# Two attention layers on one core: sums of a chunk held for a later stage, halves added by products with ones, TensorE kept busy during the first loads, and four units in the first group of scores

## The chip, the cores and the metric

The kernel runs on one core of one Trainium2 chip. The metric is the device time of one execution in microseconds (us). Several executions of each kernel were timed; "median" is over those. The span that the profile gives is about 2 us shorter than the time, because it runs from the first to the last instruction of the core. The granted clock is the share of full speed that the profile shows for TensorE's clock, 1.00 or less. PE is TensorE, PEld its weight loads, DVE is VectorE, ACT is ScalarE, POOL is GpSimd.

## The reference, cut to what matters

The input has 8 images of 64 channels and 64 x 64 = 4096 positions. Each passes through two attention layers, and all of it is in fp32.

```python
# layer 0 of one image, n = 4096 positions
f = einsum('oc,bcn->bon', Wf, xf) + bf          # 8 channels
g = einsum('oc,bcn->bon', Wg, xf) + bg          # 8 channels
hh = einsum('oc,bcn->bon', Wh, xf) + bh         # 64 channels
beta = softmax(einsum('bci,bcj->bij', f, g), axis=2)
x = x + einsum('bcj,bij->bci', hh, beta)
# layer 1
xn = group_norm(x)                              # 8 groups
q, k, v = split(w_qkv @ xn + b_qkv)             # 64 channels each
out = softmax(q k^T * c**-0.5) v
x = w_proj @ out + b_proj + x
```

So there are 16 attentions of 4096 x 4096. The division by the sum of the exponentials is done at the end, once for each chunk of queries.

## The kernel before: the parts that matter

A layer of an image is four chunks of 2 x 512 queries; a chunk is 16 key tiles; a key tile is four units, each a score product of 128 keys with 512 queries in one PSUM bank. TensorE makes the scores, ScalarE exponentiates them into one of six buffers, TensorE weighs the values with the exponentials, and VectorE adds the exponentials of each tile into a running sum. Layers are run in the order layer 0 of image 0, layer 0 of image 1, layer 1 of image 0, layer 0 of image 2, layer 1 of image 1 and so on, so only at the beginning do two layers 0 follow each other.

```python
def weigh(i, j, e, cols, now):
    ...
    at.weigh(acc, e[:, p], t, p, j == 0, j == 2 * NT - 1, cols)
    ...
    if t == 0:
        first = e
    else:
        added = vector.tensor_add(esum, first if t == 1 else esum, e).ins   # 128x2048
    if t == NT - 1:
        finished(i, now)
```

At the end of a chunk the running sum, which still has two halves p = 0 and 1, becomes one sum for each query. There are two ways. One adds the halves on VectorE and sums over the partitions by a product with ones on TensorE. The other, for chunks that are "held", is done later, on VectorE, in the next layer-1 stage; a held sum needs a buffer of its own until then.

```python
def holds(self, c):
    return self.kind == 0 and self.b > 0 and c < (1 if self.b == 1 else NC - 1)

def halves():
    ...
    vector.tensor_add(esum[:, 0], esum[:, 0], esum[:, 1])

def sums(spare):
    for h in range(2):
        for i in range(2):
            matmul(z[row : row + 32, 0:width], ones[:, 0:32],
                   esum[:, 0, h, ts(i, width)], start=True, stop=True, ...)
    nc.scalar.copy(zs, z[:, 0:width])
    ...   # four small DMAs bring the sums to 128 partitions

def finished(i, now):
    ...
    if at.kind == 1 or next_kind == 1 or held:
        ...   # halves, transposed, reciprocals, result: in the next stage
        return
    behind(halves)()
    ...       # sums, reciprocals, result: 7, 11 and 15 tiles later
```

At the start, the first 512 columns of image 0 are projected directly (`project_direct`), the other columns of the first pair of chunks by `project(0, (1,))`, and the second pair by `rest` at step 0. The first copy of values is on VectorE, all others are on ScalarE. Layer 1 needs the group norm's reciprocal root of a variance, which VectorE finds by four steps of Newton's iteration (`deviations`).

Of the kernel before, what the change touches and what calls it, by code (L numbers as in the profile page):

```python
# [9 lines left out]
F32 = mybir.dt.float32  # L10
# [58 lines left out]
def fast_path(  # L69
# [51 lines left out]

    made_last = {}
    added = None
    tight = False

    def in_order(made, engine="tensor"):

# [22 lines left out]
    def matmul(*args, **kwargs):  # L150
        in_order(nc.tensor.matmul(*args, **kwargs))  # L151

    def behind(work_):


        def made():
            with tc.issue_after(added):
                work_()

        return made  # L160
# [22 lines left out]
        return t  # L183


    w1 = const.tile([P, 2, C8], F32, name="w1")
    for i, (w, queue) in enumerate(((WfT, nc.scalar), (WgT, nc.sync))):
        for h in range(2):
# [24 lines left out]
    with tc.issue_after(masked):  # L213
# [10 lines left out]
        wfg = const.tile([P, 2, 4, C8], F32, name="wfg")  # L224
        nc.vector.tensor_copy(wfg, w1.unsqueeze(2).broadcast_to([P, 2, 4, C8]))
    wfg = wfg.rearrange("p i s c -> p (i s c)")
    fgb_low = const.tile([P, 2], F32, name="fgb_low")
    fgb, lowmask = fgb_low[:, 0:1], fgb_low[:, 1:2]
    for j in range(2):
# [20 lines left out]
    nc.vector.tensor_single_scalar(odd, lane, 1, op=ALU.bitwise_and)  # L250
    lowmask32 = const.tile([P, 1], F32, name="lowmask32")
    nc.vector.tensor_scalar(lowmask32, odd, -1.0, None, op0=ALU.mult)
    ones = const.tile([P, C], F32, name="ones")
    nc.vector.memset(ones, 1.0)


    QP = 2 * CW // P
# [67 lines left out]
    class Attention:  # L325
# [7 lines left out]

        def holds(self, c):

            return self.kind == 0 and self.b > 0 and c < (1 if self.b == 1 else NC - 1)

        def values(self, src, w, c):

            ps = pair()  # L340
            for t in range(TPC):
                for m in range(2):
                    for h in range(2):
                        matmul(
                            ps[ts(m, C), h, ts(t, C)], src[ts(h, C), ds(t * P + m * C, C)],
                            w[ts(h, C), :], start=True, stop=True,
                        )

            copy = vector.tensor_copy if self.kind == self.b == c == 0 else nc.scalar.copy
            copy(  # L350
                self.vt[:, :, ts(c, TPC), :],
                ps[:, :, 0 : TPC * C].rearrange("k p (t c) -> k p t c", c=C),
            )

        def finish(self, acc, esum, c, index):

            n = f"{self.name}_{c}"
            raw = work.tile([P, CW], F32, tag="raw", bufs=4, name=f"raw_{n}")
            other = self.total(raw, acc, index)
            zt = small.tile([P, QP], F32, tag="zt", bufs=4, name=f"zt_{n}")  # L360
            width = CW // 2
            r = four = None

            def halves():
                if other is not None:
                    vector.tensor_add(raw, raw, other)
                vector.tensor_add(esum[:, 0], esum[:, 0], esum[:, 1])

            def transposed():


                nonlocal four
                both_ = work.tile([P, 8 * QP], F32, tag="zs", name=f"part_{n}")
                part = both_[:, 0:32]
                four = both_[:, 32:].rearrange("p (a k) -> p a k", k=QP)
                vector.tensor_reduce(
                    part, esum[:, 0].rearrange("p h (i b) -> p b (h i)", b=32),
                    axis=AX.X, op=ALU.add, apply_transpose=True,
                )
                for a in range(4):  # L380
                    nc.sync.dma_start(four[:, a, :], part[ts(a, 32), :])

            def sums(spare):

                z = banks[:, spare, :]

                zs = work.tile([P, width], F32, tag="zs", name=f"zs_{n}")
                for h in range(2):
                    for i in range(2):
                        row = 32 * (2 * h + i)  # L390
                        matmul(
                            z[row : row + 32, 0:width], ones[:, 0:32], esum[:, 0, h, ts(i, width)],
                            start=True, stop=True, tile_position=(0, row),
                        )
                nc.scalar.copy(zs, z[:, 0:width])
                for h in range(2):
                    for i in range(2):
                        row = 32 * (2 * h + i)
                        nc.sync.dma_start(zt[row : row + 32, :], zs[row : row + 1, :])  # L399

            def broadcast():
                nonlocal r
                r = work.tile([P, CW], F32, tag="r", name=f"r_{n}")

            def reciprocals():
                rt = stash[:, ts(index, QP)]
                if four is not None:
                    vector.tensor_reduce(
                        zt, four.rearrange("p a k -> p k a"), axis=AX.X, op=ALU.add
                    )  # L410
                vector.reciprocal(rt, zt)
                broadcast()
                dealt = recips[index]
                nc.sync.dma_start(dealt, rt)
                for h in range(2):
                    row = dealt[ts(h, C), :].rearrange("p e -> (p e)")
                    nc.sync.dma_start(r[ts(h, C), :], row.partition_broadcast(C))

            def result():
                vector.tensor_mul(raw, raw, r)  # L420
                self.residual(raw, c)

            return halves, transposed, sums, reciprocals, result
# [52 lines left out]
    class Layer0(Attention):  # L476
# [4 lines left out]
        def before(self):  # L481



            def begin():
                if self.b == 1:
                    self.own(F32R)
                else:
                    self.parts = proj.tile([P, 2, NH], F32R, tag="fg", name=f"fg_{self.name}")
                    if self.b != 2:  # L490
                        self.own_vt()
                self.f, self.g = self.parts[:, 0, :], self.parts[:, 1, :]
                self.st = small.tile(
                    [P, NC, nc.vector.BN_STATS_DIM], F32, tag="st", name=f"st_{self.name}"
                )
                if self.b > 0:
                    self.project_all()
                else:
                    self.project_direct()
                    self.project(0, (1,))  # L500

            def rest():
                self.project(1)
                with tc.issue_after(self.sent.ins):
                    for b in (1, 2):
                        load_x(b)

            if self.b == 0:
                return [(-1, begin, True), (0, rest, True)] + [
                    (  # L510
                        (-1, 1, 5, 8)[c],
                        lambda c=c: self.values(x_tiles[0][:, ts(c, CW)], wh, c),
                        True,
                    )
                    for c in range(NC)
                ]



            s, spread = (28, 32) if self.b == 1 else (0, 28)  # L520
            return [(s, begin, True), (spread, self.spread, False)] + [
                (
                    (36, 38, 43, 45)[c],
                    lambda c=c: self.values(x_tiles[self.b][:, ts(c, CW)], wh, c),
                    True,
                )
                for c in range(NC)
            ]
# [4 lines left out]
        def home(self, c):  # L533

            if self.b > 1:
                if c == 0:
                    layers1[self.b].own(F32)
                return layers1[self.b].parts[:, c, :]
            layers0[2].own_vt()
            return layers0[2].vt.rearrange("q p t c -> q (p t c)")  # L540

        def project_direct(self):

            ps = pair()
            full = work.tile([P, 2, CW], F32, tag="full", bufs=1, name="full_direct")
            high = work.tile([P, 2, CW], F32R, tag="high", bufs=1, name="high_direct")
            for i, dst in enumerate((self.f, self.g)):
                matmul(
# [110 lines left out]
    class Layer1(Attention):  # L659
# [8 lines left out]
        def before(self):  # L668
# [32 lines left out]
            def deviations():  # L701
# [8 lines left out]
                )  # L710
                y = guess.bitcast(F32)
                w = small.tile([P, 1], F32, tag="w", name=f"w_{n}")
                for i in range(4):
                    vector.scalar_tensor_tensor(w, y, y, ve, op0=ALU.mult, op1=ALU.mult)
                    vector.tensor_scalar(w, w, -0.5, 1.5, op0=ALU.mult, op1=ALU.add)
                    vector.tensor_mul(y, y, w)
# [179 lines left out]
    def finished(i, now):  # L896
# [7 lines left out]
        if at.kind == 1 or next_kind == 1 or held:  # L904
# [4 lines left out]
            for s, u in ((0, halves), (1, transposed), (5, reciprocals), (8, result)):  # L909
                at_step(when + s, behind(u), 0)  # L910
            return
        behind(halves)()

        spare = outer[c % 2 if at.kind == 0 else 1]
        delay = 7 if at.kind == 0 else 5
# [35 lines left out]
    while i < len(seq):  # L951
# [32 lines left out]
        while u < len(units):  # L984
# [13 lines left out]
            if taken == PAIR:  # L998
                lent = 0 if room[-1] == 7 else 2
                room = [r for r in room if r not in (2 * lent + 1, 2 * lent + 2)]  # L1000
            group = list(zip(units[u : u + len(room)], room))
            u += len(group)
            for (k, t, p, h), bank in group:
# [411 lines left out]
```

## Time and profile before

| before | |
|---|---|
| median time | 3005.99 us (3005.14 to 3006.30, 4 runs) |
| span of the profile | 3004.0 us |
| first scores | 14.40 us |
| fourth group of scores | 27.20 us |
| first scores of layer 1 of image 0 | 338.95 us |
| first layer 0 after a layer 1 | 562.59 us |

Layer 1 of image 0, where the timeline has its first scores (`banks<-kq_l` of 64 x 64):

```profile
338.95 3.66 PE L151 MATMUL banks<-kq_l 64*64 64x512 f32 x32
```

The stretch between the fourth group and that mark, as one window (length, then busy us of PE, PEld, DVE, ACT, POOL, then granted clock, DMA share, GB/s):

```profile
27.20:338.95 311.75, 302.27 (x2099) 110.11 (x2097) 294.41 (x175) 251.79 (x227) 0.00 (x0) 1.00 0.11 28
```

TensorE has 9.48 us without work in it (311.75 less 302.27).

### The profile page before, as it was taken

The page shows a single profiled execution, that of the slowest core. Times are in us where ns is not written, and L with a number is a line of the kernel's source. Part 1 is how long each engine was busy: PE and PEld are TensorE (multiplying, and loading weights), DVE is VectorE, ACT ScalarE, POOL GpSimd, SP SyncE. Part 2 cuts the span into 40 slices and gives each one's busy share as a digit, 9 for nine tenths or more (in the row PEclk, how much of TensorE's full clock was granted, in tenths as well). Part 3 has the DMA queues.
Part 4 walks back from the last instruction along what each step waited for, and adds up shares of the span by engine and source line. Part 5 has one row for each costly group of instructions (what it writes and reads, how often), then busy time and mean ns, then how long its engine had stood idle before and what let it go on. Part 6 is the DMA issues. An engine that isn't in the chain of part 4 may idle for free.

```text
span 3004.0 us, 58286 instructions
## 1 busy us (share of the span) xinstructions
PE 2973.7 (99%) x25629; PEld 1078.7 (36%) x25629; DVE 2574.0 (86%) x1659; ACT 2073.0 (69%) x2019; POOL 16.1 (1%) x40
## 2 busy tenths in 40 slices
PE   8999999999999999999999999999999999999998
PEld 3333333333333333333333333333333333333333
DVE  7999986899878998789986999879997799976776
ACT  6888656786567866678666785668856688566554
POOL 2000000000000000000000000000000000000000
PEclk9999999999999999999999999999999999999999
DMA  2100100101001010010100102000020000000000
GB/s 65 43 8 15 47 16 19 30 1 44 20 20 29 1 45 19 21 28 1 49 19 20 26 1 51 16 23 22 1 52 20 19 8 1 17 24 15 9 16 13
DMA packets 77141, 66.93 MB, mean 22 GB/s; under 512 B 54048, under 2 KB 54080, under 8 KB 75088
## 3 DMA queue, kind: packets, MB, share of 16 engines
q1 hardware_dynamic: 75792, 63.01, 8.7%
q8 instruction: 202, 3.31, 0.5%
q14 instruction: 59, 0.48, 0.1%
q0 software_dynamic: 768, 0.09, 0.0%
q10 hardware_dynamic: 320, 0.04, 0.0%
HBM read 39.84 MB, written 12.32 MB: 17 GB/s over the span
## 4 chain that ended last, share of the span: by engine, by line
PE 93%; DVE 4%; issue 1%; ACT 1%; DMA 0%; SPq 0%; DVEq 0%; ACTq 0%
PE banks L151 93%; DVE esum_l L141 3%; DVE vt_l L141 1%; ACT e_l L1013 1%; DMA x<-in_x_dram 0%; DVE x L141 0%; DVE raw_l L141 0%; DVE st_l L141 0%; ACT full_l L573 0%; DVE high_l L141 0%; DVE kq_l L141 0%; DVE rt L141 0%; SPq L399 0%; DMA zt_l<-zs_l 0%; DVE w_l L141 0%
## 5 line engine op out<-in xcount | busy, mean ns | idle before, releaser
L141 DVE TENSOR_TENSOR esum_l<-esum_l,e_l 128x2048 f32<-128x2048 f32 x629 | 1438.9, 2288 | 272.0 <-ACT e_l L972 246.3
L972 ACT ACTIVATE e_l<-banks 128x1024 f32<-128x1024 f32 x1024 | 992.2, 1022 | 680.6 <-PE banks L151 680.6
L151 PE MATMUL banks<-e_l,v_l 64*64 64x512 f32 (+1 forms) x8780 | 1090.2, 586 | 0.0
L1013 ACT ACTIVATE e_l<-banks 128x2048 f32<-128x2048 f32 (+3 forms) x727 | 953.8, 1373 | 183.5 <-PE banks L151 165.9
L151 PE MATMUL banks<-kq_l 64*64 64x512 f32 (+1 forms) x8448 | 1004.4, 585 | 6.5 <-ACT e_l L1013 5.7
L151 PE MATMUL banks<-e_l,vt_l 128*64 128x512 f32 (+1 forms) x4056 | 829.8, 550 | 0.0
L141 DVE TENSOR_TENSOR kq_l<-kq_l,e_l 128x2048 f32<-128x2048 f32 x252 | 577.5, 2292 | 24.4 <-ACT e_l L1013 0.5
L151 PEld LDWEIGHTS banks<-e_l,v_l 64*64 64x64 f32 (+1 forms) x8780 | 346.9, 133 | 589.3 <-issue 490.0
L151 PEld LDWEIGHTS banks<-kq_l 64*64 64x64 f32 (+1 forms) x8448 | 326.2, 134 | 602.9 <-issue 561.8
L151 PEld LDWEIGHTS banks<-e_l,vt_l 128*64 128x64 f32 x4056 | 267.8, 136 | 467.7 <-issue 447.6
L151 PE MATMUL banks<-fg_l 32*128 32x512 f32 x1792 | 204.7, 459 | 6.2 <-ACT e_l L1013 3.1
L141 DVE TENSOR_TENSOR esum_l<-e_l,e_l 128x2048 f32<-128x2048 f32 x45 | 102.3, 2274 | 86.2 <-ACT e_l L972 86.2
L151 PEld LDWEIGHTS banks<-fg_l 32*128 32x128 f32 x1792 | 84.8, 183 | 186.8 <-ACT e_l L1013 139.8
L141 DVE TRANSPOSE_TENSOR_REDUCE part_l<-esum_l 128x32 f32<-128x1024 f32 x38 | 74.7, 1967 | 0.0
L141 DVE TENSOR_TENSOR esum_l<-esum_l 128x1024 f32<-128x1024 f32 x44 | 53.7, 1220 | 0.4
L141 DVE TENSOR_TENSOR raw_l<-raw_l,r_l 128x512 f32<-128x512 f32 x63 | 43.2, 685 | 2.1 <-DMA r_l<-recips 2.1
L141 DVE TENSOR_TENSOR kq_l<-e_l,e_l 128x2048 f32<-128x2048 f32 x18 | 41.1, 2283 | 0.0
L651 ACT COPY raw_l<-banks 128x512 f32<-128x512 f32 x32 | 18.9, 590 | 25.2 <-PE banks L151 24.3
L141 DVE TRANSPOSE_TENSOR_REDUCE part_l<-kq_l 128x32 f32<-128x1024 f32 x18 | 35.2, 1955 | 0.0
L141 DVE TENSOR_TENSOR vt_l<-vt_l,e_l 128x2048 f32<-128x2048 f32 x14 | 32.1, 2291 | 1.2
L764 ACT ACTIVATE kq_l<-banks,kqb 64x256 f32<-64x256 f32 x64 | 30.1, 470 | 1.2
L151 PEld LDWEIGHTS banks<-wh,x 64*64 64x64 f32 x1024 | 21.2, 138 | 16.7 <-issue 15.8
(127 smaller groups left out, 467.9 us busy)
## 6 DMA issues: line engine op xcount, KB each, us to landing
r_l<-recips SPq DMA_DIRECT2D x126, 128.0 KB
kq_l<-kq_l SPq DMA_DIRECT2D x64, 128.0 KB
out_dram<-raw_l SPq DMA_DIRECT2D x62, 128.0 KB
x<-in_x_dram SPq DMA_DIRECT2D x30, 256.0 KB
fg_l<-fg_sent_l SPq DMA_DIRECT2D x24, 256.0 KB
fg_l<-fg_sent_l SPq DMA_DIRECT2D x48, 128.0 KB
part_l<-part_l SPq DMA_DIRECT2D x228, 4.0 KB
fg_sent_l<-high_l SPq DMA_DIRECT2D x28, 128.0 KB
```

Source lines behind the costliest of these rows:

```text
L141: it = getattr(nc.vector, name)(*args, **kwargs)
L151: in_order(nc.tensor.matmul(*args, **kwargs))
L651: nc.scalar.copy(raw, acc[0])
L764: nc.scalar.activation(self.q[ts(h, C), cols[1]], ps[other, 1, 0:width], AF.Identity, bias=k1["kqb"][other, :],)
L972: nc.scalar.activation(e[:, p], both_ps[p], AF.Exp, scale=at.scale)
L1013: nc.scalar.activation(e.rearrange("k p h n -> k (p h) n")[:, first_ : first_ + n_, :], banks[:, bank : bank + n_, :], AF.Exp, scale=at.scale,
```

## The change

Five things are changed. (1) The two halves of a sum are no longer added on VectorE ahead of the product with ones; the product accumulates over both. (2) The first three chunks of image 1 are held in place of the first alone, two of them in a buffer that belongs to a projection later. (3) Newton's iteration takes three steps. (4) At the start, TensorE multiplies ones and weights into a bank that nobody reads until x has come; the copy of the first values goes to ScalarE; the tile of the direct projection gets another buffer; the second projection is asked for at step 2; and VectorE's instructions are held in program order (`tight`) ahead of the first chunk too (both kernels hold them so in the first eight chunks). (5) The first group of scores of a layer 0 that follows a layer 1 has four units in place of six.

```diff
-    tight = False
+    tight = True
...
+    def warm(rows, n):
+        for i in range(n):
+            matmul(banks[0:C, 7, 0:C], rows, rows, start=True, stop=True)
+    warm(ones, 18)
...
+    warm(wfg, 10)
...
-            return self.kind == 0 and self.b > 0 and c < (1 if self.b == 1 else NC - 1)
+            return self.kind == 0 and self.b > 0 and c < NC - 1
...
-            copy = vector.tensor_copy if self.kind == self.b == c == 0 else nc.scalar.copy
-            copy(
+            nc.scalar.copy(
...
-                        matmul(z[row : row + 32, 0:width], ones[:, 0:32],
-                               esum[:, 0, h, ts(i, width)], start=True, stop=True, ...)
+                for p in range(2):
+                            matmul(z[row : row + 32, 0:width], ones[:, 0:32],
+                                   esum[:, p, h, ts(i, width)],
+                                   start=p == 0, stop=p == 1, ...)
...
-                return [(-1, begin, True), (0, rest, True)] + [
+                return [(-1, begin, True), (2, rest, True)] + [
...
+            if c == 1:
+                self.free = proj.tile([P, 2, NH], F32, tag="fg", name="free")
+            return self.free[:, c - 1, :]
...
-            full = work.tile([P, 2, CW], F32, tag="full", bufs=1, name="full_direct")
+            full = ppool.tile([P, 2, 2, CW], F32, tag="e", name="full_direct")[:, 0]
...
-                for i in range(4):
+                for i in range(3):          # Newton
...
-        behind(halves)()
...
+            if u == 0 and i > 0:
+                room = room[:4]
```

More of the change, by code (lines that the diff above doesn't have):

```diff
@@ L183, in twice @@
         return t
+    ones = const.tile([P, C], F32, name="ones")
+    nc.vector.memset(ones, 1.0)
+    def warm(rows, n):
+        for i in range(n):
+            matmul(banks[0:C, 7, 0:C], rows, rows, start=True, stop=True)
+    warm(ones, 18)
     w1 = const.tile([P, 2, C8], F32, name="w1")
@@ L252, in fast_path @@
     nc.vector.tensor_scalar(lowmask32, odd, -1.0, None, op0=ALU.mult)
-    ones = const.tile([P, C], F32, name="ones")
-    nc.vector.memset(ones, 1.0)
     QP = 2 * CW // P
@@ L387, in sums @@
                 zs = work.tile([P, width], F32, tag="zs", name=f"zs_{n}")
-                for h in range(2):
-                    for i in range(2):
-                        row = 32 * (2 * h + i)
-                        matmul(
-                            z[row : row + 32, 0:width], ones[:, 0:32], esum[:, 0, h, ts(i, width)],
-                            start=True, stop=True, tile_position=(0, row),
-                        )
+                for p in range(2):
+                    for h in range(2):
+                        for i in range(2):
+                            row = 32 * (2 * h + i)
+                            matmul(
+                                z[row : row + 32, 0:width], ones[:, 0:32],
+                                esum[:, p, h, ts(i, width)],
+                                start=p == 0, stop=p == 1, tile_position=(0, row),
+                            )
                 nc.scalar.copy(zs, z[:, 0:width])
@@ L538, in home @@
                 return layers1[self.b].parts[:, c, :]
-            layers0[2].own_vt()
-            return layers0[2].vt.rearrange("q p t c -> q (p t c)")
+            if c == 0:
+                layers0[2].own_vt()
+                return layers0[2].vt.rearrange("q p t c -> q (p t c)")
+            if c == 1:
+                self.free = proj.tile([P, 2, NH], F32, tag="fg", name="free")
+            return self.free[:, c - 1, :]
         def project_direct(self):
             ps = pair()
-            full = work.tile([P, 2, CW], F32, tag="full", bufs=1, name="full_direct")
+            full = ppool.tile([P, 2, 2, CW], F32, tag="e", name="full_direct")[:, 0]
             high = work.tile([P, 2, CW], F32R, tag="high", bufs=1, name="high_direct")
```

## The prediction

> **What bounds the kernel now.** I read the page first, then busy time by stage, then the chain of waits, then the timeline of TensorE and VectorE at the places where the chain leaves TensorE.
>
> ```profile
> PE 2973.7 (99%) x25629; PEld 1078.7 (36%) x25629; DVE 2574.0 (86%) x1659; ACT 2073.0 (69%) x2019; POOL 16.1 (1%) x40
> ...
> PE 93%; DVE 4%; issue 1%; ACT 1%; DMA 0%; SPq 0%; DVEq 0%; ACTq 0%
> ```
>
> TensorE has only 30 us of idle time in 3004 us, so no change that leaves its work alone can win more than about 1%. The 4% of the chain on VectorE shows that it isn't the bound everywhere. Where, the table by stage tells (columns: length, then busy us of PE, weight load, DVE, ACT, POOL; clock; DMA).
>
> ```profile
> 28.00:62.00 34.00, 33.68 (x254) 12.62 (x254) 32.55 (x15) 28.87 (x27) 0.00 (x0) 1.00 0.39 94
> ...
> 90.00:112.00 22.00, 21.14 (x177) 7.98 (x174) 21.50 (x13) 18.86 (x17) 0.00 (x0) 1.00 0.46 121
> ...
> 187.00:225.00 38.00, 35.44 (x207) 11.95 (x203) 36.68 (x21) 29.71 (x26) 0.00 (x0) 1.00 0.03 8
> ...
> 238.00:270.00 32.00, 28.55 (x192) 10.28 (x188) 30.47 (x31) 24.12 (x22) 0.00 (x0) 1.00 0.07 17
> 270.00:314.00 44.00, 42.75 (x324) 16.05 (x322) 39.92 (x24) 36.30 (x37) 0.00 (x0) 1.00 0.08 19
> 314.00:340.00 26.00, 26.00 (x205) 9.59 (x201) 24.96 (x13) 18.94 (x20) 0.00 (x0) 1.00 0.04 11
> ```
>
> From 28 to 314 us the first two images' layer 0 runs alone. Summed over all windows of that stretch TensorE is busy 276.8 of 286 us: 9.2 us of stalls. VectorE is busy nearly without a break. From 314 us layer 1 joins and TensorE stalls no more. The timeline of VectorE says what fills it:
>
> ```profile
> 63.13 1.23 DVE L141 TENSOR_TENSOR esum_l<-esum_l 128x1024 f32<-128x1024 f32 x1
> ...
> 82.27 0.20 DVE L141 RECIPROCAL stash<-zt_l 128x8 f32<-128x8 f32 x1 [1.33 <-DMA zt_l<-zs_l]
> ...
> 285.69 0.20 DVE L141 RECIPROCAL stash<-zt_l 128x8 f32<-128x8 f32 x1 [2.72 <-DMA zt_l<-zs_l]
> ```
>
> Besides its 2.29 us add per key tile (2.39 us from start to start), it has one 1.23 us "halves" add per chunk and waits for sums coming back by DMA. TensorE needs 3.82 us per group of seven units in undisturbed stretches, four units to a key tile: 2.18 us. So VectorE falls behind by 0.2 us per tile, plus its extras, until the six buffers of exponentials are full; then TensorE waits. The other loss is the start:
>
> ```profile
> 7.26 3.75 PE L151 MATMUL banks<-x,direct 128*128 128x512 f32 x4 [7.26 <-DMA x<-in_x_dram]
> ...
> 20.59 3.68 PE L151 MATMUL banks<-e_l,vt_l 128*64 128x512 f32 x8
> ...
> 24.20 1.20 PE L151 MATMUL banks<-fg_l 32*128 32x512 f32 x7
> ...
> 25.33 1.94 PE L151 MATMUL banks<-e_l,vt_l 128*64 128x512 f32 x8
> ```
>
> The same eight weighing records take 3.68 us at 20.59 and 1.94 us at 25.33. The windows give a granted clock of 0.50 from 16 to 24 us and 1.00 from 26.
>
> **What the Trainium skill says.** "TensorE: Matmul & The Clock Gate", Part 1, "What's actually happening": the array runs at half clock until about 3.4 us of activity, and falls back after an idle window. The trace agrees: 3.68 against 1.94 us is the factor, and the clock falls again after the gaps at 12.8 to 15.5 us. "VectorE: DVE Perf Modes", "The TRN2 errata": an fp32 tensor_tensor of N columns takes (N+151)/0.96 ns: 2291 for 2048 and 1224 for 1024; the trace has 2288 and 1220, so an add can only be removed or moved, not sped up. "Perfetto Trace Analysis", "Optimization Strategy": a kernel can have regimes with different contended engines; here a VectorE regime of 286 us stands before a TensorE regime of 2690.
>
> **The change part by part.**
>
> (1) Halves by ones products. Four chunks of image 0 lose the halves add; the product with ones gets eight matmuls for four. VectorE: 4 x 1.2 = 4.8 us less. TensorE: the end of the kernel runs 16 records of this kind in 1.07 us against 0.64 for eight, so 0.43 us more each, 1.7 us in all.
>
> (2) Sums held. Chunks 1 and 2 of image 1 keep their sums in a layer-0 projection buffer that is free by then and are finished in the layer-1 stage. Out of the stretch before 314 us go two halves adds (2.4), the reciprocal and its 2.72 us wait (2.9), and the result of chunk 1 (0.68 + 0.75 + 0.69 = 2.1): 7.4 us. TensorE loses two ones products, 1.2 us. The layer-1 stage gets two halves, two transposing reductions at 1.97, two results and small reductions: about 11 us of VectorE.
>
> (3) Newton's iteration runs three times for four: 0.64 us per image (three operations from 244.06 to 244.70). Only the first is on the path: TensorE waits 1.14 us at 245.50 for the normalised x behind it. So VectorE loses 4.8 + 7.4 + 0.6 = 12.8 us before 314 us.
>
> (4) The start. Products of ones keep TensorE active while x loads, so the direct projection should run at full clock, about 1.8 us for 3.75. The copy of the first values goes from VectorE to ScalarE (0.69 us out of the chain of the g projection). The direct tile no longer shares a buffer with the next projection, for which ScalarE waited 2.63 us at 14.38. My chain: first product done 8.2, ScalarE to 8.9 and 9.9, VectorE's casts and masks to 11.4; first scores at 11.4 instead of 14.40. Exponentials of tile 0 from 12.1, of tile 1 (after a 0.6 copy) to 16.5; third group of scores at about 18 instead of 24.20. Then a transfer: the 64 KB copies of the projection took from 17.62 to 25.34 (7.7 us); now they start at about 13.5 and land at 21.2, and tile 4, in the fourth group, needs them. So the fourth group at about 21.3 instead of 27.20: 5.9 us. VectorE's first add waits behind the second projection's cast, which waits for the same transfers: 21.2 + 2.0 = 23.2 instead of 27.28: 4.1 us.
>
> (5) Four units in the first group, at six joints from layer 1 to a later layer 0. One joint before:
>
> ```profile
> 562.59 0.73 PE L151 MATMUL banks<-fg_l 32*128 32x512 f32 x6
> 563.25 1.95 PE L151 MATMUL banks<-e_l,v_l 64*64 64x512 f32 x16
> 565.15 0.51 PE L151 MATMUL banks<-fg_l 32*128 32x512 f32 x4
> 566.06 0.50 PE L151 MATMUL banks<-fg_l 32*128 32x512 f32 x2 [0.41 <-ACT e_l L1013]
> 566.49 2.80 PE L151 MATMUL banks<-e_l,vt_l 128*64 128x512 f32 x12
> 569.22 0.73 PE L151 MATMUL banks<-fg_l 32*128 32x512 f32 x7
> ```
>
> The second group waits 0.41 us for the exponentials of units five and six, and the split costs some 0.3. With four units the second group finds six free banks. But then only four units are there to weigh (1.7 us) while ScalarE has six to exponentiate (1.88 + 1.03 = 2.9 us), so the third group waits about 0.75 us. A layer still takes 38 groups either way, by the built instruction order. Worth nothing: 0.0 us, give or take 0.3 at each of six joints.
>
> **Sum.** Two clocks run through the first stretch. By VectorE: 12.8 less work and 4.1 earlier start, 16.9 us. By TensorE: 5.9 earlier; 9.2 of stalls and about 3 of split score groups (0.50 + 0.50 for 0.73, some ten times) can go; 1.7 - 1.2 = 0.5 is added: 17.6 us. Neither reaches its own limit, because the two now want almost the same time and a stall on one side is not made up by the other: VectorE will still find the 1.33 us wait for the sums and the 2.23 us wait for the projection of image 1 at 89 us, and TensorE will still stall at some of them. I take 3 us off for that. Then layer 1 of image 0: VectorE gets 11 us more there, in front of 64 tiles that leave it 3.43 - 2.39 = 1.04 us each. I take 1.5 us for stalls in its first dozen tiles. 17 - 3 - 1.5 = 12.5 us, so 3006 - 12.5 = 2993.5 us.
>
> **The rivals.** (a) The moved work comes back. Layer 1 of image 0 starts with VectorE late by nearly its whole buffer, and four chunks to finish at 5.7 us each in about twelve tiles: 23 + 29 us of adds against 41 us. If TensorE stalls for that, up to 6 us are lost: 2999. Against: in the later stages four chunks are finished in just that place, VectorE runs without a break from 699 to 787 us, and TensorE has no stall in the chain there (566 to 931 is one piece of TensorE). (b) The clock falls back. TensorE has gaps while ScalarE works on the first exponentials (from 12.8 to 14.0 in my chain); before, gaps of this kind brought 0.50 back for some 9 us. Then weighing tile 0 takes 3.7 again, the fourth group slips to 22.5 or 23, and 1 to 2 us are lost: 2995. (c) VectorE ceases to be a bound and TensorE runs the stretch at its own pace: 17.6 less nothing: 2988.5. For it: the savings lie just behind the chunk ends, where the stalls at 111.9, 189.3 and 249.7 are. (d) The first transfers hold everything: x lands at 7.26 whatever is done, and the 7.7 us of copies stand between the first scores and tile 4. If the sending is slower when it falls beside the loads of constants, the start is worth 3 instead of 5.9: 2996.
>
> **Range and chances.** The terms are 4 to 6 for the start, 6 to 11 for the stretch after it, 0 to 6 given back in layer 1, and -2 to +2 for the joints. That gives 2988 to 2999.5. Two per cent are 60 us, twice all the idle time of TensorE, so faster by over 2% can't come of this change (0.002); slower by over 2% would take a new wait in every layer, which nothing in the order shows (0.005).
>
> **What would show it.** Granted clock near 1.00 from 8 us on and the direct products in under 2 us; first scores at 11 to 12; the first key-tile add near 23; layer 1 beginning at 298 to 303 instead of 313.6; busy TensorE over 98% between 28 and 300; no halves add at a chunk end of image 0 and four such adds after layer 1 begins; about 0.4 to 0.8 us of waiting at each joint, one group later than before. It is wrong in (2) if TensorE shows stalls behind ScalarE waiting for VectorE after layer 1 begins, and in (5) if the distance between the joints (368.5 us, as in 564.99 to 933.48) moves by more than 0.5 us: each such us counts six times.

## The result, and the profile after

The changed kernel took 2994.64 us (median of 4 runs, 2994.55 to 2994.72). The ratio is 0.9963 (95% interval 0.9945 to 0.9980). That is 11.35 us, or 0.4%; 12.5 us had been predicted.

| mark | before | after | won up to here |
|---|---|---|---|
| first scores | 14.40 | 11.58 | 2.82 |
| fourth group of scores | 27.20 | 21.49 | 5.71 |
| first scores of layer 1 of image 0 | 338.95 | 327.55 | 11.40 |
| first layer 0 after a layer 1 | 562.59 | 551.18 | 11.41 |
| span | 3004.0 | 2992.8 | 11.2 |

So half came from the first 27 us, half from the 300 us after it, and at most 0.2 us came or went in the remaining 2665 us. First the page of the changed kernel, busy times and chain:

```profile
PE 2972.9 (99%) x25693; PEld 1080.3 (36%) x25693; DVE 2566.9 (86%) x1634; ACT 2072.8 (69%) x2031; POOL 15.9 (1%) x40
...
PE 98%; ACT 1%; DVE 1%; issue 0%; DMA 0%; SPq 0%; DVEq 0%; ACTq 0%
```

The chain stays on TensorE for 98% where it was 93%, and VectorE's 4% is now 1%. That is the change's intent. TensorE's timeline at the start of the changed kernel, which answers to the lines of the start in the prediction:

```profile
7.24 1.96 PE L151 MATMUL banks<-x,direct 128*128 128x512 f32 x4 [0.85 <-DMA x<-in_x_dram]
...
11.58 0.51 PE L151 MATMUL banks<-fg_l 32*128 32x512 f32 x4 [0.91 <-ACT full_l L586]
...
14.06 0.63 PE L151 MATMUL banks<-fg_l 32*128 32x512 f32 x4 [1.26 <-ACT e_l L1027]
14.62 1.99 PE L151 MATMUL banks<-x,wfg 64*64 64x512 f32 x8
16.54 2.50 PE L151 MATMUL banks<-e_l,vt_l 128*64 128x512 f32 x8
18.96 0.73 PE L151 MATMUL banks<-fg_l 32*128 32x512 f32 x7
```

The direct products take 1.96 us for 3.75, as predicted. But eight weighing records take 2.50 us at 16.54, where 1.94 is the time at full clock, and the eight projections take 1.99 where (in the experiment without a fall) 1.09 is. The windows give the clock: it falls all the same, only for a shorter time.

```profile
8.00:12.00 4.00, 3.09 (x43) 1.36 (x41) 2.73 (x5) 3.02 (x4) 4.00 (x8) 1.00 0.38 75
12.00:16.00 4.00, 2.72 (x48) 1.05 (x44) 1.51 (x2) 3.67 (x4) 3.89 (x10) 0.79 0.18 49
16.00:20.00 4.00, 4.00 (x21) 1.17 (x19) 0.00 (x0) 2.21 (x3) 4.00 (x9) 0.79 0.36 108
```

The stretch to layer 1, again as one window between the same two marks:

```profile
21.49:327.55 306.06, 302.40 (x2107) 110.26 (x2105) 286.38 (x163) 251.32 (x226) 0.00 (x0) 0.99 0.11 27
```

It is 5.69 us shorter. TensorE's idle time went from 9.48 to 3.66 us, which is 5.82 us; its busy time rose by 0.13. VectorE does 8.03 us less in it. Of the idle time that is left, 0.80 us lie at 22.79 and 2.80 in one place, where layer 1 of image 0 gets its first projection:

```profile
236.03 0.66 PE L151 MATMUL banks<-kq_l,wkq_wvp 64*64 64x256 f32 x8 [0.50 <-DVE kq_l L141]
236.62 2.37 PE L151 MATMUL banks<-e_l,v_l 128*64 128x512 f32 x12
240.19 0.51 PE L151 MATMUL banks<-kq_l 32*128 32x512 f32 x4 [1.21 <-ACT e_l L1027]
241.31 0.86 PE L151 MATMUL banks<-kq_l 32*128 32x512 f32 x2 [0.61 <-ACT e_l L1027]
242.65 0.52 PE L151 MATMUL banks<-kq_l 32*128 32x512 f32 x1 [0.48 <-ACT kq_l L777]
243.10 4.84 PE L151 MATMUL banks<-e_l,v_l 128*64 128x256 f32 x16
```

Four waits of 2.80 us together, and then sixteen weighing records in 4.84 us, where other sixteens of this kind take 3.23. The windows of the same place show why:

```profile
240.00:243.00 3.00, 1.72 (x7) 0.73 (x7) 2.86 (x2) 2.42 (x6) 0.00 (x0) 1.00 0.00 0
243.00:245.00 2.00, 2.00 (x9) 0.90 (x10) 1.94 (x1) 2.00 (x2) 0.00 (x0) 0.50 0.00 0
245.00:247.00 2.00, 2.00 (x10) 0.56 (x8) 1.90 (x2) 0.84 (x1) 0.00 (x0) 0.65 0.00 0
```

The clock fell to half, which the profile of the kernel before doesn't show there, although its four waits (1.14, 1.21, 0.61 and 0.48) were longer: 1.6 us of the gain are given back here. Without this the stretch's busy time would have gone down by some 1.5 us: TensorE starts 85 groups of scores in it in place of 90 (a count of the timeline), since a group is cut short less often.

### The profile page after: what moved, and what is told of

Same layout as the page of the kernel before. It is cut to its first block, busy times and chain, and to the rows that moved or that the text cites. A ratio compares the mean times of both kernels' runs of the same rounds, so it can differ in the third digit from the quotient of the medians. Undisturbed runs are those within 1.5% of the kernel's fastest.

```text
span 2992.8 us, 58406 instructions
## 1 busy us (share of the span) xinstructions
PE 2972.9 (99%) x25693; PEld 1080.3 (36%) x25693; DVE 2566.9 (86%) x1634; ACT 2072.8 (69%) x2031; POOL 15.9 (1%) x40
## 4 chain that ended last, share of the span: by engine, by line
PE 98%; ACT 1%; DVE 1%; issue 0%; DMA 0%; SPq 0%; DVEq 0%; ACTq 0%
PE banks L151 98%; ACT e_l L1027 1%; DVE free L141 0%; DVE raw_l L141 0%; DMA x<-in_x_dram 0%; ACT kq_l L777 0%; DVE rt L141 0%; SPq L198 0%; DVE raw_end L141 0%; DVE w_l L141 0%; ACT full_l L586 0%; DVE guess_l L141 0%; ACT kq_l L772 0%; SPq L168 0%; ACT raw_end L460 0%
## 5 line engine op out<-in xcount | busy, mean ns | idle before, releaser
L141 DVE TENSOR_TENSOR esum_l<-esum_l,e_l 128x2048 f32<-128x2048 f32 x601 | 1374.3, 2287 | 262.6 <-ACT e_l L984 240.1
L141 DVE TENSOR_TENSOR free<-free,e_l 128x2048 f32<-128x2048 f32 x28 | 64.2, 2291 | 2.6
L141 DVE TENSOR_TENSOR esum_l<-esum_l 128x1024 f32<-128x1024 f32 x38 | 46.3, 1218 | 0.0
```

What stands on the lines that cost most here:

```text
L141: it = getattr(nc.vector, name)(*args, **kwargs)
```

## The experiments

Each edit is made to the changed kernel unless said otherwise. All gave correct results. They came in three sets, each on one chip; the kernel before had medians of 3006.14, 3005.44 and 3005.44 us there. "Loss" is the median less the changed kernel's 2994.64 (or 2995.02, its second run); parts of a microsecond aren't to be trusted in it, since a kernel's own executions differ by up to 4.8 us. The unaltered changed kernel ran beside the others in the second set only. No run takes back `tight` alone, so its worth isn't known.

### The changed kernel once more

No edit. This gives a second profile, beside those of the other sets.

> The changed kernel unaltered, on this chip, as the mark for the other runs: 2994.6, and up to 1.5 us more in executions in which the clock falls for longer between the first scores (the run with the halves back had tile 0 weighed in 3.68 us at the same place where the changed kernel took 2.50).

Measured: 2995.02 us (2993.44 to 2995.85). In this profile the clock fell for longer at the start (tile 0 weighed in 3.68 us, fourth group at 22.9 instead of 21.49) and again at 243 us (4.92 us for sixteen records); layer 1 began at 329.06. So the same kernel, with the same order of instructions, reaches this mark up to 1.5 us apart, through the clock alone. Marks are compared below with a profile of a like start.

### Without the early products

```diff
-    warm(ones, 18)
-    warm(wfg, 10)
```

> The changed kernel without its 28 early products. Clock theory: the direct products go back from 1.96 to about 3.75 us, the weighing of the first tiles to about 3.7 us a tile, and TensorE arrives in the stretch 3.5 to 5 us later: 2998 to 2999.5. Rival (the order of the start does it, the clock only the direct products): 1.8 us later, 2996.4. Second rival (VectorE bounds the stretch, and its first add hangs on the copies of the projection): most of it is swallowed, under 1 us.

Measured: 2995.55 us (2995.44 to 2996.79), a loss of 0.5 to 0.9. So the early products win little, as the second rival had it. The profile shows why:

```profile
7.24 3.75 PE L151 MATMUL banks<-x,direct 128*128 128x512 f32 x4 [7.24 <-DMA x<-in_x_dram]
...
13.11 1.10 PE L151 MATMUL banks<-fg_l 32*128 32x512 f32 x4 [0.23 <-DVE fg_l L141]
...
16.66 1.09 PE L151 MATMUL banks<-x,wfg 64*64 64x512 f32 x8
17.68 1.94 PE L151 MATMUL banks<-e_l,vt_l 128*64 128x512 f32 x8
19.54 0.77 PE L151 MATMUL banks<-fg_l 32*128 32x512 f32 x7
```

The first scores come 1.5 us later, as the slow direct products make them. But the array then stays at full clock, where the changed kernel's falls, and by the third group of scores only 0.6 us are left of the 1.5 (19.54 against 18.96). What the early products win, the fall after them takes back in part. Layer 1 begins at 328.78: 1.2 us behind the first profile of the changed kernel and 0.3 ahead of its second, so the early products are worth less than what the clock makes of two executions behind them.

### The early products in the kernel before

```diff
 # in the kernel before
+    warm(ones, 18)
...
+    warm(wfg, 10)
```

> The kernel before with the 28 early products alone. Clock theory: the first scores come 1.8 us earlier (12.6 for 14.40) and the group at 35.06 comes 3 to 4 us earlier; but VectorE bounds the stretch here, and its first add can come earlier only by what the copies of the projection allow, about 2 us: 3003.5 to 3004.5. Rival (the start goes through to the end undiminished): 3002.

Measured: 3006.61 us (3005.90 to 3006.91) against 3006.14, no gain. The first scores stood at 14.20, although the direct projection ended 1.3 us earlier (9.70 for 11.01). It isn't a clean test: with VectorE not held in program order, the edit also changed which instruction VectorE took first, and the copy of the values went ahead of the casts that the scores wait for. Nor does it show that the early products bring nothing: its profile has two falls of the clock, at 224.73 and 252.09 (sixteen records in 4.92 us for 3.23 each time), that the profile of the kernel before doesn't have. They cost 3.4 us together, and layer 1 began only 0.7 us later (339.68 for 338.95).

### The start's old order, with the early products kept

```diff
-            nc.scalar.copy(
+            copy = vector.tensor_copy if self.kind == self.b == c == 0 else nc.scalar.copy
+            copy(
...
-                return [(-1, begin, True), (2, rest, True)] + [
+                return [(-1, begin, True), (0, rest, True)] + [
...
-            full = ppool.tile([P, 2, 2, CW], F32, tag="e", name="full_direct")[:, 0]
+            full = work.tile([P, 2, CW], F32, tag="full", bufs=1, name="full_direct")
```

> The changed kernel with the three order changes of the start undone (second projection before the second group, first values copied by VectorE, direct tile in the shared buffer), products of ones kept. Theory: ScalarE waits again for VectorE at the first projection (2.6 us before) and the copies of the projection start about 2 us later: 2 to 3 us slower, 2996.6 to 2997.6. Rival (the clock alone gives the 5.5 us of the start): within 0.5 us of 2994.6.

Measured: 2998.94 us (2997.92 to 2999.70), a loss of 3.9 to 4.3. This is most of what the start is worth:

```profile
11.63 0.50 PE L151 MATMUL banks<-fg_l 32*128 32x512 f32 x2 [0.91 <-DVE fg_l L141]
12.76 0.50 PE L151 MATMUL banks<-fg_l 32*128 32x512 f32 x2 [0.63 <-ACT full_l L587]
15.70 1.98 PE L151 MATMUL banks<-x,wfg 64*64 64x512 f32 x8 [2.44 <-DVE vt_l L141]
...
20.02 3.68 PE L151 MATMUL banks<-e_l,vt_l 128*64 128x512 f32 x8
23.63 1.09 PE L151 MATMUL banks<-fg_l 32*128 32x512 f32 x7
```

The first scores come as early as in the changed kernel (11.63), and yet the third group comes only at 23.63, near the 24.20 of the kernel before. The second projection stands ahead of the second scores and waits 2.44 us for a PSUM bank that the copy of values on VectorE has not yet emptied. Not all of this is the order: the clock fell for longer behind that wait (tile 0 weighed in 3.68 us for 2.50). Beside the second profile of the changed kernel, whose fall at the start was as long, the fourth group is 3.6 us later (26.52 for 22.93). So the order makes most of the gain at the start; the loss was larger than either forecast.

### Two of the three parts of that order, alone

The copy of the first values back on VectorE:

```diff
-            nc.scalar.copy(
+            copy = vector.tensor_copy if self.kind == self.b == c == 0 else nc.scalar.copy
+            copy(
```

> The changed kernel with only the copy of the first values back on VectorE. In the run with the whole start order undone TensorE waited 2.44 us for that copy. Theory: with the second projection after the second group nothing waits for that copy before tile 0 is weighed, ScalarE is even 0.6 us ahead: within 0.7 us of the changed kernel. Rival (the copy is what held the old order): 2 us slower.

Measured: 2996.94 us (2996.83 to 2997.00), a loss of 1.9 to 2.3. The second half of the values waits 2.31 us for the bank (`<-DVE vt_l`), the second scores come at 15.53 for 14.06 and the third group at 21.11 for 18.96. The rival was right.

The tile of the direct projection back in the shared buffer:

```diff
-            full = ppool.tile([P, 2, 2, CW], F32, tag="e", name="full_direct")[:, 0]
+            full = work.tile([P, 2, CW], F32, tag="full", bufs=1, name="full_direct")
```

> The changed kernel with only the direct tile back in the buffer that the projections use. Theory: the projection's ScalarE step can begin only when VectorE has made g (10.68 + 0.75), so about 11.5 for 10.33, and all copies of the projection, VectorE's first add with them, come 1.2 us later; 1 us slower. Rival (ScalarE takes the copy of the values in that time and nothing is lost): 0.

Measured: 2996.41 us (2995.66 to 2997.20), a loss of 1.4 to 1.8. The first scores come in two pairs again, 11.61 and 12.74, since ScalarE cannot write the next projection until the direct tile has been read, and the third group comes at 21.46 (20.39 in the second profile of the changed kernel, whose fall of the clock was as long). The third part, the later second projection, was not run alone; together the three lose 3.9 to 4.3, so 0.2 to 0.6 us are left for it and for what they do jointly.

### Halves back on VectorE

```diff
-                for p in range(2):
-                            matmul(..., esum[:, p, h, ts(i, width)], start=p == 0, stop=p == 1, ...)
+                            matmul(..., esum[:, 0, h, ts(i, width)], start=True, stop=True, ...)
...
+        behind(halves)()
```

> The changed kernel with the halves adds of image 0's four chunks back on VectorE and four products of ones in place of eight. Theory (VectorE is still nearly full between 28 and 240 us): 4.8 us more on VectorE, 1.7 us less on TensorE, of which 2 to 4 us come out at the end: 2996.6 to 2998.6. Rival (VectorE is no longer a bound, TensorE's 1.7 us count): 2993.

Measured: 2997.28 us (2996.14 to 2997.64), a loss of 2.3 to 2.6. Its start had the long fall of the clock, and there was a second one, here at 221 us (sixteen records in 4.92 us), so its marks are compared with the second profile of the changed kernel, which had two of the same size: layer 1 began at 330.72 against 329.06, a loss of 1.7 us. In the time and by the mark, then, part (1) is worth about 2 us, of the 4.8 - 1.7 = 3.1 that VectorE's saving and TensorE's cost would give. The waits show the mechanism. The first line is from the kernel before, the others are from this run; the last is the window from the fourth group to layer 1:

```profile
189.30 0.50 PE L151 MATMUL banks<-kq_l 32*128 32x512 f32 x1 [1.11 <-ACT e_l L1013]
...
185.28 0.49 PE L151 MATMUL banks<-kq_l 32*128 32x512 f32 x1 [1.11 <-ACT e_l L1026]
...
22.96:330.72 307.76, 301.53 (x2074) 109.44 (x2073) 289.91 (x166) 251.50 (x226) 0.00 (x0) 0.99 0.11 27
```

The kernel before has five waits between 100 and 230 us (0.86, 0.74, 1.11, 0.85 and 0.60). The changed kernel has none of them, and here all five are back (0.86, 0.75, 1.11, 0.87 and 0.61). Against the second profile of the changed kernel, between the same marks, TensorE has 2.56 us more idle time and 0.93 less work. So VectorE's halves made these waits.

### One chunk held

```diff
-            return self.kind == 0 and self.b > 0 and c < NC - 1
+            return self.kind == 0 and self.b > 0 and c < (1 if self.b == 1 else NC - 1)
```

> The changed kernel with only chunk 0 of image 1 held, as before; the others by eight products of ones. VectorE gets back a reciprocal with its wait and one result, about 5 us, TensorE two products of ones, 2 us, before layer 1 begins. Theory (VectorE is late by its whole buffer only up to about 243 us, after that TensorE sets the pace): 2 to 3.5 us slower, 2996.6 to 2998.1. Rival (VectorE bounds to the end of the stretch): 5 us, 2999.6. Second rival (the moved work costs as much in layer 1 as it saved): 2994.6.

Measured: 2997.75 us (2997.57 to 2997.81), a loss of 2.7 to 3.1; layer 1 begins at 330.60. Holding two more sums is the largest single part after the start's order. But it isn't VectorE that makes most of this loss:

```profile
21.60:330.60 309.00, 304.81 (x2146) 111.67 (x2145) 290.34 (x167) 251.36 (x227) 0.00 (x0) 0.99 0.11 28
```

From the fourth group to layer 1 it needs 2.94 us more than the changed kernel (306.06). TensorE's work is 2.41 of them, of which the two products with ones of 1.07 us each are 2.1. Its idle time grew by only 0.53, in two waits at 266.67 and 285.93, although VectorE had 3.96 us more to do.

### Four steps of Newton's iteration

```diff
-                for i in range(3):
+                for i in range(4):
```

> The changed kernel with a fourth Newton step. Theory: 0.64 us of VectorE in front of the normalised x of image 0, where TensorE waits 0.50 us at 236.03; the wait becomes 1.14 and the time 0.6 us more; the later images show nothing. Rival (VectorE's lateness swallows it): 0.

Measured: 2995.59 us (2992.02 to 2996.80), a loss of 0.6 to 1.0, but with a spread wider than that. The line that waits for it is clearer than the time:

```profile
235.90 0.66 PE L151 MATMUL banks<-kq_l,wkq_wvp 64*64 64x256 f32 x8 [1.14 <-DVE kq_l L141]
```

1.14 us for 0.50, which is the 0.64 of one step, all of it on the path. Its clock differs too. At 243 us it fell for longer (sixteen records in 5.74 us). At the start, which is the changed kernel's own, it didn't fall at all, and the third group came 1.5 us earlier than in the first profile of the changed kernel (17.46 for 18.96).

### Six units in the first group

```diff
-            if u == 0 and i > 0:
-                room = room[:4]
```

> The changed kernel with six units in the first group of a later layer 0. Theory (the wait only moves by a group): distance of the joints 368.5 us as in both kernels, time within 0.5 us of the unaltered one beside it. Rival (the four units win what the prediction did not see): six times 0.3 us, 1.8 us slower.

Measured: 2994.51 us (2992.28 to 2995.35), no loss. The third group of the first joint and of the next stood at 553.94 and 922.45, 368.5 us apart, as in the kernel before. With four units, the same two joints look like this in the changed kernel:

```profile
553.75 0.73 PE L151 MATMUL banks<-fg_l 32*128 32x512 f32 x6 [0.18 <-ACT e_l L1027]
...
556.28 0.51 PE L151 MATMUL banks<-fg_l 32*128 32x512 f32 x4
557.15 0.50 PE L151 MATMUL banks<-fg_l 32*128 32x512 f32 x3 [0.36 <-ACT e_l L1027]
```

```profile
924.77 0.50 PE L151 MATMUL banks<-fg_l 32*128 32x512 f32 x4
```

One wait of 0.41 us and a split of four and two units have become two waits of 0.18 and 0.36 us and a split of four and three. 556.28 to 924.77 is 368.49 us. Part (5) is worth nothing.

### More products in the gaps, and two Newton steps

The two falls of the clock are part of what the changed kernel still loses, so this one puts products that nobody reads into the two gaps among the first scores, and takes one more step from the chain that ends in the gap at 236 us.

```diff
-                for i in range(3):
+                for i in range(2):
...
             at_step(s, u, buffer)
+    warm(wfg, 6)
+    at_step(1, lambda: warm(wfg, 8), 0)
```

> An attempt at a faster one: six and eight more products of nothing in TensorE's gaps before the first and second scores, and two Newton steps for three. Clock theory: no half clock before 28 us in any execution, so the start is at its best (third group at 17.5, fourth at 21.3) and does not vary; Newton 0.6 less: 2992.5 to 2993.5 with a spread under 2 us. Rival (the products fall in the way of the scores): 2995.

Measured: 2992.19 us (2990.48 to 2993.88, 5 runs), ratio 0.9958 (0.9944 to 0.9971) to the kernel before. It is the fastest of all, 2.5 us ahead of the changed kernel by the medians. Its start:

```profile
10.61 0.91 PE L151 MATMUL banks<-wfg 128*64 128x64 f32 x12
11.61 0.51 PE L151 MATMUL banks<-fg_l 32*128 32x512 f32 x4
...
12.74 1.15 PE L151 MATMUL banks<-wfg 128*64 128x64 f32 x16
14.09 0.51 PE L151 MATMUL banks<-fg_l 32*128 32x512 f32 x4 [0.20 <-ACT e_l L1029]
14.56 1.09 PE L151 MATMUL banks<-x,wfg 64*64 64x512 f32 x8
15.58 1.94 PE L151 MATMUL banks<-e_l,vt_l 128*64 128x512 f32 x8
17.45 0.76 PE L151 MATMUL banks<-fg_l 32*128 32x512 f32 x7
```

The first and second scores come when they did in the changed kernel (11.61 and 14.09), for TensorE had been waiting there anyway. But what follows runs at full clock, 1.09 and 1.94 us, and the third group comes at 17.45 for 18.96. From the fourth group (20.01) to layer 1 (323.74) it needs 303.73 us for 306.06:

```profile
20.01:323.74 303.73, 300.64 (x2106) 109.80 (x2104) 286.50 (x161) 251.35 (x226) 0.13 (x1) 1.00 0.11 27
```

1.76 us less of TensorE's busy time and 0.57 less of idle time: in this execution, the fastest of its five, the clock did not fall at 243 us (sixteen records at 240.91 took 3.23). The other four took 1.5 to 3.4 us longer, with a mean granted clock of 0.998 or 0.999; they left no trace, so that the fall came back in them is likely but not shown. The two edits were not run apart. That the filling keeps the clock up is likely but not shown: both profiles with it have no fall at the start, but neither has the one with four Newton steps, without filling; the other five profiles with that start have one.

### The same, with the normalised x of image 0 on GpSimd

```diff
-                vector.tensor_scalar(
+                engine = nc.gpsimd if self.b == 0 else vector
+                engine.tensor_scalar(
                     self.x[:, cols], x_tiles[self.b][:, cols], mu, self.a,
```

> As the run before it, and image 0's normalised x made by GpSimd in place of VectorE: 4 x 0.54 us of VectorE less, but the first of them lies in the chain before the projection that TensorE waits for. Theory (VectorE's lateness makes the 1.21 + 0.61 us of stalls near 240 us): they shrink by 0.5 us or more, 2991.5 to 2993. Rival (GpSimd is slower at it than 0.55 us by several us and TensorE waits for the projection): 2994 to 2997.

Measured: 2992.28 us (2992.11 to 2993.73), no gain over the one above. VectorE loses its 0.55 us, but the operation takes much longer on GpSimd, 3.1 us on the mean of four, and TensorE waits for it:

```profile
237.57 1.13 PE L151 MATMUL banks<-kq_l,wkq_wvp 64*64 64x256 f32 x8 [3.43 <-POOL kq_l L739]
238.63 4.53 PE L151 MATMUL banks<-e_l,v_l 128*64 128x512 f32 x12
```

One long wait takes the place of three short ones (1.14, 0.61 and 0.49 us in the run above), and the clock falls behind it (twelve records in 4.53 us for 2.37).

## Why the prediction was right, and where its steps were not

The time was right to 1.1 us, and the mechanism was right in its main point: VectorE held TensorE up before layer 1 of image 0, and taking work from it there pays: the run with the halves back brings the same waits again. But several terms were off, and errors stood against each other.

(1) Halves by products: 3.1 us were assumed (4.8 of VectorE less 1.7 of TensorE), 1.7 to 2.6 were measured.

(2) Sums held: this was the term most over-sized. 7.4 us of VectorE were to leave the stretch, and with TensorE's 1.2 they were to count almost wholly; undoing it costs 2.7 to 3.1, and 2.1 of this is TensorE's work in two products with ones, not VectorE's time. In the whole stretch VectorE's busy time fell by 8.03 us where (1), (2) and (3) had 12.8, 2.7 of it a wait; and of these 8.03 the stretch became only 5.69 shorter, since VectorE's idle time in it rose from 17.34 to 19.68 us: it was no longer the later of the two everywhere. (VectorE trails TensorE, at whose marks the stretch is cut, so its part is not exact.) That is rival (c) in part, and the 3 us taken off for "neither reaches its own limit" were of the right kind, if too few.

(3) Newton's step: 0.64 us, all on the path, shown by the wait of 1.14 against 0.50.

(4) The start: 5.9 us at the fourth group, 5.71 measured; the first add on VectorE at 23.2, 22.72 measured. The sum was right and its reason was not: the fourth group did not wait for the transfers. In the changed kernel TensorE had no wait from 14.06 until that group; and where the clock stayed up, in the run with more products in the gaps, the group came before the transfers had all landed:

```profile
20.01 0.50 PE L151 MATMUL banks<-fg_l 32*128 32x512 f32 x4
...
20.84 0.69 DVE L141 CAST high_l<-full_l 128x1024 fp32r<-128x1024 f32 x1 [7.20 <-DMA fg_l<-high_l]
```

That 21.3 and 21.49 agree is luck. Nor does VectorE's first add pass on its lateness, as the prediction's clock of VectorE has it: without the early products it came 3.1 us later (25.84 for 22.72), and layer 1 only 1.2. "Granted clock near 1.00 from 8 us on" failed: it was 0.79 from 12 to 20 us, as rival (b) had it, and the early products were worth under 1 us. The reordering, by the run with the old order, was worth 3.9 to 4.3, a longer fall of the clock included. The transfers' 7.7 us were right to half a microsecond: VectorE's second cast waits for them until 20.79, where 21.2 was predicted.

(5) Four units: nothing predicted, nothing found, and the distance of the joints stayed at 368.5 us. The waits were smaller than the 0.75 us that the prediction had for the third group (0.18 and 0.36), which is within its 0.3 a joint.

The sum put 17 less 3 us before layer 1 and took 1.5 off for stalls in it. Measured: 11.4 before it and 0 in it. The mark "layer 1 beginning at 298 to 303 instead of 313.6" was a mistake in reading: those 313.6 us are only the end of the last place where VectorE held TensorE up, in layer 0 of image 1, and layer 1 of image 0 really begins at 338.95 us. The 1.5 us failed for another reason. VectorE does have the four finishes to do behind 327.55 us, and this is how it takes them in the changed kernel:

```profile
324.85 0.69 DVE L141 CAST high_l<-full_l 128x1024 fp32r<-128x1024 f32 x1 [4.42 <-ACT full_l L621]
...
333.64 1.22 DVE L141 TENSOR_TENSOR vt_l<-vt_l 128x1024 f32<-128x1024 f32 x1
...
341.30 1.22 DVE L141 TENSOR_TENSOR free<-free 128x1024 f32<-128x1024 f32 x1
...
351.21 1.22 DVE L141 TENSOR_TENSOR free<-free 128x1024 f32<-128x1024 f32 x1
...
362.89 1.22 DVE L141 TENSOR_TENSOR esum_l<-esum_l 128x1024 f32<-128x1024 f32 x1
```

It comes to that stage having had 4.42 us of idle time, so it isn't late by its whole buffer as rival (a) assumed, and the finishes come one at a time, 8 to 12 us apart, among the adds of the tiles. TensorE runs from the mark to the next joint without a wait. The moved work was free. What took the gain down to 11.4 can be read from TensorE's side of the sum. Predicted were 5.9 at the start, 9.2 of stalls, about 3 of split groups, less 0.5 for products: 17.6. Measured are 5.7, 5.8, 1.9 (what is left of TensorE's busy time, a difference) and 0.4, and another 1.6 lost to the fall of the clock at 243 us, where the prediction had not looked for one: 11.4. The largest miss is that all 9.2 us of stalls "can go": 3.66 us of idle time stayed, and the three waits behind the projection at 236 us (1.21, 0.61 and 0.48) are as long as before the change.

The 17 us of the parts were thus 5.6 too high. The 4.5 us taken off made up for most of that, though 1.5 of them stood for stalls that didn't come. So it is partly luck that the number is within 1.1 us.

Adding up the losses: order at the start 4.1, early products 0.7, halves 2.4, sums held 2.9, Newton 0.8 (each the middle of its two figures), four units 0. That is 10.9 of 11.35 us. The parts needn't add exactly, since VectorE's lateness and the clock join them, and since undoing the held sums brings products of eight matmuls where the kernel before had four.

What stays open is why the clock fell at 243 us in some executions and not in others. Nothing here controls it: the run with the old start order had four waits of the same length there (0.51, 1.21, 0.61 and 0.48) and no fall.

## What to carry to other kernels

When two engines bound a stretch in turn, mark a few events that exist in both kernels and difference them; here the marks showed what each part of this change was worth, and that the moved work cost nothing. Before crediting a gain at the start to a warm clock, put the old order of instructions back with the clock kept warm: here the order was worth some 4 us and the early products under 1, since the clock fell again behind them; where it stayed up, the third group came 2.1 us earlier than without them (17.45 for 19.54). And once the waits are short, look at what follows them: a cluster of waits can cost more in the clock behind it than in itself, and products that nobody reads, in the gaps among the first scores, did not delay the scores.

## What the Trainium skill lacked or had wrong

- "TensorE: Matmul & The Clock Gate", Part 1, has the clock fall after an idle window of about 3.4 us. Here it fell to 0.50 though no wait was longer than 1.21 us (2.80 us of waits between 235.5 and 243.1), and at the start behind waits of 0.91 and 1.26 us; in the kernel before, 3.44 us of waits in the same place brought no fall. The page's "A second HAM failure mode: psum-queue depth-cycling" does name short idle times between groups of matmuls, but not how much of them counts, and these runs don't settle it; that it is different from one execution to the next agrees with what the page says of a window that runs freely.
- Not reached here: "GPSIMD Engine Reference", "4.1 Engine selection", has elementwise operations of one input on GpSimd at roughly line rate, and those of two inputs at about half of VectorE's speed. A tensor_scalar of 128x512 fp32 with one tensor input and two values per partition took 3.1 us there on the mean (median 2.8) against 0.55 us on VectorE, five times as long; GpSimd's durations are rough in a profile, but TensorE's wait of 3.43 us for it says the same. VectorE was adding two tensors beside it (233.27 to 246.67), and the page's "8. Key points" names contention with such instructions, so the run doesn't show the line rate itself to be wrong.
